# A fused two-layer block on one core: root of the first norm, first masks, one load and the last feature chunk changed, and the written order of all steps replaced

## The chip, the cores and the metric

The kernel runs on one NeuronCore of a Trainium2 chip. The metric is device time in microseconds (us) for one launch. A profiled execution also gives a span, from its first to its last instruction, and every start time below counts from the start of that span. The engines are PE (TensorE, matmuls and transposes), ACT (ScalarE), DVE (VectorE), POOL (GpSimd) and SP (SyncE, which here only issues DMAs). Each engine works through its own instructions in order and waits on semaphores for the others.

## The reference

The input x is 4 x 1024 tokens of 128 features, fp32. There are two layers, each of the form x + s * silu(g), where s comes from an attention and g from a feed-forward network, both fed by a layer norm without learned factors.

```
xn = layernorm(x)                                     # (x - mean) / sqrt(var + 1e-5)
# layer 0, attention: 16 heads of 8, causal, at most 64 back, with a linear bias per head
k, q, v = split(xn @ w_kqv)
s = softmax(q k / sqrt(128) + slope * (key - query), masked) v
# layer 0, feed-forward: weights mixed anew for each of the 4 batches
gate = mean over tokens of (relu(xn gate_w1 + gate_b1) gate_w2 + gate_b2)     # 8 shares
mW1 = W1 + sum_e gate_e TW1_e;  mW2 = W2 + sum_e gate_e TW2_e
g = gelu_tanh(xn mW1 + mb1) mW2 + mb2
x = x + s * silu(g);  xn = layernorm(x)
# layer 1, attention: over the 4 batches at each of the 1024 sites, 16 heads of 8
s = softmax(q k + gated relative bias) v, times Wo, plus bo
# layer 1, feed-forward, hidden size 512; the weights are -1, 0 or 1, with a scale per output
h = silu(w1 xn) * (w2 xn);  h = gelu(h1 h);  h = gelu(h2 h);  g = w3 h
out = x + s * silu(g)
```

## The kernel before

**Units and steps.** The 4096 tokens are worked on in eight units of 512 (`UNITS`: batch and half), numbered 0 to 7. All work is cut into some 1,400 small steps, each a Python function with a short name; `x.02` is the exponential (`x`) of unit 0, tile 2. The string `ORDER` lists all the steps, and `program` calls them in that order. The scheduler is told to keep that order on PE, ACT, DVE and POOL, so each engine's queue is exactly the order in which the steps that use it are written. DMAs are issued by SP in the same way; a DMA issue waits on a semaphore that an earlier transfer raises (there are eight for these queues, taken in turn), so the position of a load in the list also sets which earlier transfer its issue waits for. `PLACES` fixes by hand which buffer each tile takes: eight big SBUF tiles, seven PSUM banks (`ps_M`; digits 3 to 6 only after the scores have ended), four 2 KB tiles (`t2k`) and three streaming tiles (`tw`).

**The bar in ORDER.** What stands before `|` runs first. It ends with a flag (`VF`) that tells whether the fast arithmetic is safe for these weights: norms of the query and key weights (`VN`), and sums over the low halves of the layer-1 weights (`CK.0` to `CK.3`; CK.0 on DVE, the others on ACT). Every engine reads the flag and branches; the fast branch runs the rest, and in the profile it is the one taken. The other branch is an exact version of the same.

**Steps that the change and the prediction speak of, with their lines.** Norm: `ls` statistics (DVE, L411, L413), `lp` root (L418 adds epsilon on DVE or POOL, L419 raises to -0.5 on POOL), `n` scaling (DVE, L426, four instructions), `k` transposes (PE, L432), `K` copy to `xn` (ACT, L437). Layer 0: `q` queries, keys, values (PE, L534 to L537; queries first), `kp` and `kc` older and new keys (POOL; DVE, L555), `FI` ones for the softmax sums (POOL), `m` masked queries (ACT, L571, one 512-wide piece for each of four groups, read from PSUM), `v` values (DVE, L579), `s` scores (PE: L590 adds the additive mask tile `unseen` by small bf16 matmuls, L600 the products), `x` exponential (ACT, L638), `o` weighing (PE, L653), `c`, `p`, `d` copy, turn and divide; `A`, `AR`, `B`, `BP`, `C` the gate; `RW` row weights (PE, L399, from the tile `sb`, then DVE); `E` mixing (DVE, L518: 00 to 07 for mW1, 08 to 0f for mW2 of batch 0); `T` streams expert weights in; `f`, `F`, `g`, `G`, `GS`, `r` the feed-forward. The scores of one tile fill four PSUM banks and there is one such set, so s of the next tile waits for x of the one before it.

Layer 1: `wa`, `wb` and `W`, `U`, `V` are the gated product (PE L756; ACT L767 with a Silu for units 3, 6, 7, L769 with a Tanh for the others; DVE). `ha`, `hb` with `hg`, `hH`, `hL`, and `ia`, `ib` with `ig`, `gH`, `gL`, are the two hidden layers: PE (L810), gelu in place in PSUM (ACT, L820 and L831), a rounded high part (ACT, L826 and L837) and the remainder (DVE, L797). High and low parts go through PE as two fp32r matmuls each, which together keep fp32 accuracy because the weights are exact in fp32r. `j` multiplies by w3 (PE, L845), `J` is the last silu (ACT, L857), `jt` turns it (PE, L864), `y` multiplies (DVE, L869), `Y` adds x and stores (POOL, or DVE for unit 7, L874). `a`, `aq`, `av`, `ag`, ... `ay` are the second attention.

**Table loads.** ACT loads a table whenever its next function is not in the one it has; each such load is one instruction. Exp, gelu, tanh-gelu and silu need different ones; copies, relu and tanh do not force a load.

Of the kernel before, what the change touches and what calls it, by code (L numbers as in the profile page):

```python
# [11 lines left out]
F32 = mybir.dt.float32  # L12
# [9 lines left out]
P = 128  # L22
B, S, D = 4, 1024, 128
H, HD = 16, 8
W = 64
# [27 lines left out]
def constants():  # L53
# [26 lines left out]
    ls.00 lp.00 0. 0. 0. 0. 0. ls.10 lp.10 n.00 k.00 K.00 n.10 q.0 CK.1 m.00 m.03 FI. m.02 kc.0 kp.0 A.00 v.00 v.01 k.10  # L80
    v.02 m.01 K.10 s.00 CK.0 x.00 A.01 AR.01 RW. s.01 VN. AR.00 B.0 CK.3 BP.0 C.0 H.0 E.00 o.00 x.01 s.02 E.01 E.02 CK.2
    E.03 ls.30 E.04 VP. x.02 o.01 E.05 s.03 c.01 D.0 lp.30 x.03 p.01 E.06 d.01 HD.0 E.07 o.02 n.30 o.03 k.30 c.03 kp.1
    p.03 VF. d.03 K.30 | L.1 ls.20 f.10 F.10 q.1 f.00 m.10 lp.20 kc.1 m.12 F.00 m.13 v.11 S.4 f.01 A.11 m.11 f.02 T.00
    n.20 v.10 v.12 F.01 T.01 ls.60 AR.11 f.11 F.02 k.20 S.0 s.10 ls.40 F.11 K.20 T.11 E.08 E.09 f.03 E.0a T.12 S.1 f.12
    lp.40 E.0b E.0c A.10 x.10 AR.10 o.10 E.0d B.1 E.0e s.11 F.03 E.0f n.40 f.13 BP.1 ls.50 lp.60 F.12 C.1 x.11 g.00 T.10
    lp.50 F.13 g.01 E.10 E.11 L.2 k.40 E.12 o.11 n.60 s.12 g.10 G.0 GS.0 n.50 x.12 g.11 E.13 K.40 ls.70 c.11 E.14 k.60
    s.13 r.0 K.60 x.13 A.21 E.15 G.1 ls.01 k.50 p.11 T.16 K.50 o.12 T.13 lp.01 E.16 E.17 T.14 d.11 T.15 E.18 AR.21 o.13
    c.13 D.1 f.20 q.2 F.20 H.1 f.30 E.19 n.01 kc.2 k.01 HD.1 m.20 T.25 m.22 E.1a F.30 f.21 K.01 f.31 m.21 F.21 E.1b F.31
    S.2 f.22 E.1c m.23 kp.2 XH.0 E.1d v.21 f.23 f.32 F.22 F.23 F.32 XL.0 v.20 v.22 wa.00 W.00 U.00 wa.01 wb.00 W.01 V.00
    s.20 wb.01 wa.02 U.01 V.01 T.17 A.20 E.1e E.1f x.20 AR.20 W.02 WH.00 wb.02 lp.70 B.2 s.21 x.21 T.20 g.20 T.24 U.02  # L90
    V.02 wa.03 WH.01 BP.2 WL.00 W.03 C.2 S.3 s.22 o.20 U.03 E.28 E.29 p.13 x.22 n.70 wb.03 o.21 GS.1 s.23 V.03 E.20 d.13
# [12 lines left out]
    m.52 F.43 g.41 ia.20 d.43 s.50 ib.20 G.4 ia.21 k.11 E.36 GS.4 E.3e ib.21 x.50 r.4 K.11 ls.41 ia.22 lp.41 ig.20 ig.21
    n.41 ib.22 gH.20 ig.22 gL.20 gH.21 gL.21 gH.22 s.51 o.50 f.60 gL.22 f.61 F.60 E.37 f.62 F.61 F.62 k.41 E.3f K.41
    XH.4 XL.4 f.50 f.51 F.50 F.51 f.52 F.52 f.53 wa.40 F.53 W.40 f.63 g.50 U.40 wb.40 n.31 F.63 V.40 g.51 wa.41 x.51 G.5
    s.52 WH.40 kp.6 o.51 wa.42 W.41 U.41 wb.41 V.41 a.00 x.52 W.42 s.53 aq.00 WL.40 av.00 wa.43 wb.42 c.51 WH.41 U.42
    p.51 x.53 V.42 o.52 d.51 W.43 WL.41 GS.5 U.43 o.53 c.53 wb.43 WH.42 ia.23 WL.42 V.43 ib.23 p.53 WH.43 d.53 ig.23 q.6
    WL.43 ha.40 kc.6 gH.23 m.60 gL.23 hb.40 j.20 v.60 ha.41 r.5 m.61 v.61 ls.51 hb.41 hg.40 m.62 hH.40 m.63 j.21 hg.41
# [38 lines left out]

DIRECT = (3, 6, 7)


AHEAD = ("FI", "q", "kp", "kc", "m", "v", "s", "x", "o", "c", "p", "d")


PLACES = {
    "big": (
        "0123456780325416724531806738426710526370847015623701601505842374206142658371437121268263756047510763"
        "48253017620317485"  # L160
# [7 lines left out]
        "01230123012301230123012301203120302130321"  # L168
    ),
    "tw": (  # L170
        "012201010200210120212010"
    ),
}

# [952 lines left out]
```

## Time and profile before

| | |
|---|---|
| median of 3 runs | 419.1 us (418.81 to 420.6) |
| the profiled execution: time, span | 418.97 us, 416.9 us |
| granted TensorE clock | 0.994 |
| busy: PE, ACT, DVE, POOL | 395.4, 352.3, 329.1, 165.8 us |
| table loads on ACT | 73, 1283 ns each |
| DMA | 26.42 MB, most of it in the first 25 and around 34 to 100 us |

Of the profile's views, the page gives busy time by engine and the span in 40 slices of 10.4 us (a digit is the busy share in tenths). The chain follows the work that ended last back from the end: start, duration, engine and line. The timeline lists instructions in order of their start, merged where neighbours are alike: start, busy time, engine, line, operation, output and input, shape, count, and in square brackets how long the engine stood idle before it and what ended that. ACT_TABLE_LOAD is a table load. A matmul of fp32 operands shows as two instructions.

### The profile page before, as it was taken

The numbers are of one execution on the slowest core, as the hardware profiler recorded it, in microseconds if no ns is written. First come the engines' busy times: TensorE is split into PE (matmuls) and PEld (weight loads), VectorE is DVE, ScalarE is ACT, GpSimd is POOL, SyncE is SP. The second block draws the span as 40 slices with busy tenths as digits, with TensorE's granted clock in tenths as the row PEclk, the third lists the DMA queues.
The fourth block names the chain that finished last, engine by engine and source line by source line (L and its number), as shares of the span: only waits on it lengthen the run. The fifth ranks groups of instructions, "written<-read, shape, count | busy, mean of one in ns | idle before, by whom it ended". The sixth has DMA issues, their size and how long they took to land.

```text
span 416.9 us, 11388 instructions
## 1 busy us (share of the span) xinstructions
PE 395.4 (95%) x4800; PEld 281.6 (68%) x4800; DVE 329.1 (79%) x704; ACT 352.3 (85%) x489; POOL 165.8 (40%) x186
## 2 busy tenths in 40 slices
PE   7779999999999999999999999999998998999992
PEld 3445686587767676757786678666786876788881
DVE  6687999787859985344565699799899999999992
ACT  1867997998979999798988899999979898988973
POOL 5012154257211530221442253462565564555462
PEclk9999999999999999999999999999999999999997
DMA  7926544332014441000000000000000000000013
GB/s 278 350 99 240 217 132 151 108 108 93 6 50 129 130 163 39 2 2 2 3 1 3 2 2 0 3 2 2 2 0 0 3 0 0 2 1 25 2 75 109
DMA packets 8891, 26.42 MB, mean 63 GB/s; under 512 B 1248, under 2 KB 2048, under 8 KB 8448
## 3 DMA queue, kind: packets, MB, share of 16 engines
q1 hardware_dynamic: 8112, 23.79, 16.7%
q10 hardware_dynamic: 720, 1.84, 1.2%
q8 instruction: 39, 0.64, 0.6%
q14 instruction: 20, 0.16, 0.1%
HBM read 23.52 MB, written 2.10 MB: 61 GB/s over the span
## 4 chain that ended last, share of the span: by engine, by line
PE 72%; ACT 14%; DVE 5%; DMA 4%; issue 3%; POOL 0%; SPq 0%; ACTq 0%; DVEq 0%; POOLq 0%
PE ps_M L810 21%; PE ps_S L600 7%; PE ps_M L756 7%; PE ps_M L696 6%; PE ps_O L653 6%; PE ps_M L713 6%; PE ps_M L898 5%; PE ps_M L845 3%; PE ps_S L590 2%; ACT big L638 2%; DMA g<-in_l1h 2%; DVE mw L518 2%; ACT L820 2%; PE ps_M L432 1%; PE ps_M L670 1%
## 5 line engine op out<-in xcount | busy, mean ns | idle before, releaser
L810 PE MATMUL ps_M<-big,l1h 128*128 128x512 f32 x512 | 130.1, 399 | 2.6 <-ACT ps_M L477 1.0
L810 PEld LDWEIGHTS ps_M<-big,l1h 128*128 128x128 f32 x512 | 94.1, 188 | 26.8 <-issue 2.0
L638 ACT ACTIVATE big<-ps_S 128x2048 f32<-128x2048 f32 x32 | 60.2, 1880 | 13.0 <-PE ps_S L600 12.9
L797 POOL TENSOR_TENSOR big<-t2k,big 128x512 fp32r<-128x512 f32 x32 | 44.6, 1402 | 52.5 <-ACT big L788 39.3
L797 DVE TENSOR_TENSOR big<-ps_M,big 128x512 fp32r<-128x512 f32 x64 | 43.1, 684 | 8.7 <-ACT big L837 4.5
L600 PE MATMUL ps_S<-big,k 32*64 32x256 f32 (+1 forms) x768 | 36.5, 462 | 1.0 <-issue 1.0
L419 POOL TENSOR_TENSOR rstd<-rstd,power 128x4 f32<-128x4 f32 x16 | 18.3, 1145 | 47.5 <-DVE rstd L418 46.7
L518 DVE SCALAR_TENSOR_TENSOR mw<-tw,gr,mw 128x512 f32<-128x512 f32 x42 | 36.1, 869 | 0.5
L653 PEld LDWEIGHTS ps_O<-big,vb 128*32 128x32 f32 x2048 | 29.8, 110 | 9.2 <-issue 7.2
L653 PE MATMUL ps_O<-big,vb 128*32 128x64 f32 x2048 | 34.0, 220 | 0.6 <-ACT big L638 0.6
L756 PE MATMUL ps_M<-xh,l1w 128*128 128x512 f32 x64 | 31.7, 495 | 1.6 <-ACT t2k L767 1.6
L696 PE MATMUL ps_M<-xn,mw 128*128 128x512 f32 x64 | 31.4, 608 | 0.8 <-DVE inv L682 0.6
L713 PEld LDWEIGHTS ps_M<-mw,big 128*128 128x128 f32 x256 | 29.8, 192 | 2.5 <-issue 1.1
L984 POOL TENSOR_TENSOR big<-big 128x512 f32<-128x512 f32 x16 | 22.4, 1407 | 22.8 <-DVE big L974 22.8
L713 PE MATMUL ps_M<-mw,big 128*128 128x128 f32 x256 | 30.9, 277 | 0.0
L898 PE MATMUL ps_M<-wa,xn 128*128 128x416 f32 x64 | 26.5, 523 | 1.2 <-ACT vb L910 1.1
L728 POOL TENSOR_TENSOR g<-g,s 128x512 f32<-128x512 f32 x8 | 11.5, 1435 | 38.6 <-ACT g L723 30.4
L600 PEld LDWEIGHTS ps_S<-big,k 32*64 32x64 f32 x768 | 18.6, 130 | 11.6 <-issue 8.8
L756 PE MATMUL ps_M<-xl,l1w 128*128 128x512 f32 x64 | 25.2, 394 | 0.0
L782 DVE SCALAR_TENSOR_TENSOR t2k<-ps_M,halved,t2k 128x512 f32<-128x512 f32 x20 | 14.9, 748 | 12.0 <-PE ps_M L756 11.7
L820 ACT ACTIVATE ps_M<-ps_M,vec 128x512 f32<-128x512 f32 x32 | 21.2, 667 | 3.2 <-PE ps_M L810 3.1
L451 POOL TENSOR_TENSOR xl<-xn,xh 128x512 fp32r<-128x512 f32 x8 | 11.4, 1420 | 31.6 <-DVE xh L443 26.1
(185 smaller groups left out, 840.8 us busy)
## 6 DMA issues: line engine op xcount, KB each, us to landing
tw<-in_tw SPq DMA_DIRECT2D x24, 512.0 KB, 4.0
big<-in_tw SPq DMA_DIRECT2D x2, 1024.0 KB, 7.1
out<-xn SPq DMA_DIRECT2D x7, 256.0 KB, 2.0
g<-in_l1h ACTq DMA_DIRECT2D x2, 512.0 KB, 7.9
g<-in_l1h SPq DMA_DIRECT2D x2, 512.0 KB, 8.6
x<-in_tw SPq DMA_DIRECT2D x2, 512.0 KB, 4.7
x<-in_x SPq DMA_DIRECT2D x1, 1024.0 KB, 6.8
x<-in_x ACTq DMA_DIRECT2D x2, 256.0 KB, 3.8
```

Of the source, the lines that this page charges most:

```text
L518: DVE.scalar_tensor_tensor(m, part, made["gr", b][:, e:e + 1], base if e == 0 else m, ALU.mult, ALU.add)
L600: PE.matmul(sp[rows, j, :, q0:q0 + n], lhsT=k[r, key:key + W], rhs=qm[r, :, t * P + q0:t * P + q0 + n], start=bool(exact), stop=bool(exact ...
L638: ACT.activation(pr, sp, AF.Exp)
L653: PE.matmul(op[32 * j:32 * j + 32, part, qs], lhsT=vb[:, col:col + 32], rhs=pr[:, j, g, qs], start=(odd + i + g == 0), stop=(odd + i + g = ...
L696: PE.matmul(hp, lhsT=made["mixed", b][0][:, c * P:(c + 1) * P], rhs=xn[:, b, cx], start=True, stop=True)
L713: PE.matmul(op[:, i, :], lhsT=hid[:, c, i * P:(i + 1) * P], rhs=m2[:, c * D:(c + 1) * D], start=(c + i == 0), stop=(c + i == FC + 2))
L756: PE.matmul(p, lhsT=wt[name][:, c * P:(c + 1) * P], rhs=m, start=(n == 0), stop=(n == len(both) - 1))
L797: engine.tensor_tensor(made[key + "l", u][:, c, :], made[key + "v", u, c], made[key + "h", u][:, c, :].bitcast(F32), ALU.subtract)
L810: PE.matmul(made[name, u, c], lhsT=wt[name][:, i, c * P:(c + 1) * P], rhs=m[:, i, :], start=(n + i == 0), stop=(last and i == FC - 1))
L820: ACT.activation(full, full, AF.Gelu, scale=v("h1s", c))
L898: PE.matmul(mp[:, 0:N_ALL], lhsT=xn[:, b, place(sl)], rhs=wa[:, 0:N_ALL], start=True, stop=True)
L984: POOL.tensor_tensor(pv[:, t:t + 2, 0:2, :], pv[:, t:t + 2, 0:2, :], pv[:, t:t + 2, 2:4, :], ALU.add)
```

## The change

1. **Order.** All of `ORDER` is new, and `PLACES` with it. The diff shows its beginning up to a little past the bar, and its end. Which steps stand before the bar is the same, apart from the new `M` steps and `kp.1`, which goes behind it.
2. **Root.** Only for the first norm (unit 0, first layer): Sqrt of the variance plus epsilon on ACT (epsilon from a new tile set by POOL), then a reciprocal on DVE. The warming instruction on ACT, which loaded a table with a copy, is now a Sqrt. Exp therefore needs a load of its own before x.00.
3. **Masks of unit 0.** `m.0g` writes only the 128 columns that s.00 reads; a new step `M.0g` writes the other 384.
4. **Load.** The DMA of `unseen` is issued behind `wg` and ahead of a raw h1 half, instead of behind `tb`.
5. **Last chunk.** For unit 7, chunk 3 (`LAST`), the second gelu writes an fp32 SBUF tile; its high part and remainder are not made, and `j.73` is one fp32 matmul (two instructions) instead of two fp32r ones.

```diff
 ORDER = """
-    ls.00 lp.00 0. 0. 0. 0. 0. ls.10 lp.10 n.00 k.00 K.00 n.10 q.0 CK.1 m.00 m.03 FI. m.02 kc.0 kp.0 A.00 v.00 v.01 k.10
-    v.02 m.01 K.10 s.00 CK.0 x.00 A.01 AR.01 RW. s.01 VN. AR.00 B.0 CK.3 BP.0 C.0 H.0 E.00 o.00 x.01 s.02 E.01 E.02 CK.2
-    E.03 ls.30 E.04 VP. x.02 o.01 E.05 s.03 c.01 D.0 lp.30 x.03 p.01 E.06 d.01 HD.0 E.07 o.02 n.30 o.03 k.30 c.03 kp.1
-    p.03 VF. d.03 K.30 | L.1 ls.20 f.10 F.10 q.1 f.00 m.10 lp.20 kc.1 m.12 F.00 m.13 v.11 S.4 f.01 A.11 m.11 f.02 T.00
...
-    aT.6 y.20 j.62 jt.00 aU.6 jt.50 gH.72 aD.71 ay.5 af.6 at.7 gL.63 y.50 aT.7 aU.7 jt.10 j.63 J.60 ay.6 gL.70 af.7 y.00
-    gL.71 ia.73 ib.73 Y.50 ig.73 ay.7 Y.20 U.63 y.10 jt.30 gL.72 gH.73 jt.60 y.30 gL.73 j.70 j.71 y.60 j.72 Y.00 Y.10
-    Y.30 Y.60 j.73 J.70 jt.70 y.70 J.71 jt.71 y.71 U.73 Y.70 Y.71
+    0. ls.00 lp.00 n.00 0. ls.10 0. 0. k.00 0. K.00 q.0 m.00 m.03 m.02 M.00 m.01 M.03 lp.10 VN. M.01 kc.0 M.02 n.10 FI.
+    CK.0 A.00 k.10 RW. v.01 kp.0 v.00 s.00 K.10 x.00 A.01 AR.01 AR.00 v.02 B.0 s.01 H.0 BP.0 o.00 C.0 CK.3 E.00 E.01
+    E.02 E.03 E.04 ls.30 lp.30 D.0 x.01 s.02 o.01 CK.1 x.02 HD.0 s.03 n.30 E.05 CK.2 c.01 p.01 VP. x.03 E.06 o.02 VF.
+    E.07 o.03 c.03 k.30 d.01 K.30 p.03 d.03 | T.00 f.10 f.00 ls.20 F.00 lp.20 T.01 q.1 f.11 n.20 F.10 L.1 T.10 kp.1 m.10
+    f.01 kc.1 k.20 v.10 F.11 m.13 F.01 f.02 A.11 K.20 A.10 F.02 AR.11 T.12 f.12 m.11 m.12 f.03 E.08 E.09 E.0a E.0b E.0c
+    AR.10 s.10 E.0d E.0e f.13 v.11 B.1 E.0f ls.60 F.12 F.03 BP.1 g.00 g.01 C.1 lp.60 T.11 x.10 v.12 s.11 E.10 n.60 F.13
+    E.11 g.10 G.0 o.10 T.13 x.11 GS.0 E.12 E.13 s.12 E.14 E.15 E.16 E.17 x.12 T.14 g.11 r.0 ls.40 o.11 S.1 E.18 s.13
+    c.11 G.1 f.20 x.13 lp.40 ls.01 p.11 lp.01 o.12 o.13 E.19 k.60 D.1 d.11 T.15 E.1a n.01 F.20 c.13 S.0 n.40 f.21 E.1b
...
+    gL.63 ay.5 gH.70 aT.6 y.50 aD.70 j.62 ig.72 aU.6 at.7 j.63 gH.71 jt.00 af.6 gL.70 aT.7 J.60 Y.50 ay.6 aU.7 y.00
+    jt.20 Y.00 jt.30 gL.71 U.33 y.20 j.70 Y.20 af.7 jt.60 ia.73 gH.72 ib.73 j.71 ay.7 y.30 y.60 gL.72 Y.30 jt.10 Y.60
+    j.72 y.10 ig.73 j.73 J.70 gL.73 jt.70 gH.73 U.63 Y.10 J.71 jt.71 y.70 y.71 Y.70 Y.71
...
 
@@ -151,24 +151,27 @@
 DIRECT = (3, 6, 7)
 
 
-AHEAD = ("FI", "q", "kp", "kc", "m", "v", "s", "x", "o", "c", "p", "d")
+LAST = (7, 3)
+
+
+AHEAD = ("FI", "q", "kp", "kc", "m", "M", "v", "s", "x", "o", "c", "p", "d")
 
 
 PLACES = {
...
 }
@@ -259,6 +262,7 @@
     nc.sync.dma_start(out=raw["h2"][:, 0:2 * F], in_=a["l1h2"][:, 0:2 * F])
     nc.scalar.dma_start(out=raw["h2"][:, 2 * F:4 * F], in_=a["l1h2"][:, 2 * F:4 * F])
     nc.sync.dma_start(out=wg, in_=a["wg"])
+    nc.sync.dma_start(out=unseen, in_=a["unseen"])
     nc.sync.dma_start(out=raw["h1"][:, 0:2 * F], in_=a["l1h1"][:, 0:2 * F])
     nc.scalar.dma_start(out=raw["h1"][:, 2 * F:4 * F], in_=a["l1h1"][:, 2 * F:4 * F])
     nc.sync.dma_start(out=sb, in_=a["sb"])
@@ -266,7 +270,6 @@
     nc.sync.dma_start(out=raw["w1"], in_=a["l1w1"])
     nc.sync.dma_start(out=raw["w2"], in_=a["l1w2"])
     nc.sync.dma_start(out=tb.rearrange("p c e -> p (c e)"), in_=a["tb"])
-    nc.sync.dma_start(out=unseen, in_=a["unseen"])
     nc.sync.dma_start(out=w1, in_=a["w1"])
 
     def v(name, i=0, n=1):
@@ -284,6 +287,8 @@
     POOL.memset(power, -0.5)
     one = const.tile([P, 1], F32, tag="one", name="one")
     POOL.memset(one, 1.0)
+    eps = const.tile([P, 1], F32, tag="eps", name="eps")
+    POOL.memset(eps, 1e-5)
     flag = tmp.tile([1, 1], I32, tag="flag", name="flag")
     made = {"nrm": small([P, 2 * H + 4], "nrm")}
 
@@ -315,7 +320,7 @@
     nc.sync.dma_start(out=w2, in_=a["w2"])
     nc.sync.dma_start(out=vec[:, early_n:V_N], in_=a["vec"][:, early_n:V_N])
     warm = const.tile([P, 1], F32, tag="warm", name="warm")
-    ACT.copy(warm, one)
+    ACT.activation(warm, one, AF.Sqrt)
     in_order = {mybir.EngineType.PE, mybir.EngineType.Activation, mybir.EngineType.DVE, mybir.EngineType.Pool}
 
     def tokens(u):
@@ -415,6 +420,10 @@
         @step("lp")
         def ln_power(u, i):
             rstd = made["rstd", u, i] = small([P, 4], "rstd")
+            if (u, i) == (0, 0):
+                ACT.activation(rstd, made["mv", u, i][:, :, 1], AF.Sqrt, bias=eps)
+                DVE.reciprocal(rstd, rstd)
+                return
             (POOL if i else DVE).tensor_scalar(rstd, made["mv", u, i][:, :, 1], 1e-5, None, ALU.add)
             POOL.tensor_tensor(rstd, rstd, power, ALU.pow)
 
@@ -568,7 +577,12 @@
         def mask(u, g):
             if ("qm", u) not in made:
                 made["qm", u] = big((P, 4, U))
-            ACT.activation(made["qm", u][:, g, :], made["qp", u], AF.Copy, scale=mpart[:, g:g + 1])
+            cols = slice(0, P if u == 0 else U)
+            ACT.activation(made["qm", u][:, g, cols], made["qp", u][:, cols], AF.Copy, scale=mpart[:, g:g + 1])
+
+        @step("M")
+        def mask_rest(u, g):
+            ACT.activation(made["qm", u][:, g, P:U], made["qp", u][:, P:U], AF.Copy, scale=mpart[:, g:g + 1])
 
         @step("v")
         def value(u, i):
@@ -794,6 +808,8 @@
                 return
             if c == 0:
                 made[key + "l", u] = big((P, FC, U), wide)
+            if (key, u, c) == ("l", *LAST):
+                return
             engine.tensor_tensor(made[key + "l", u][:, c, :], made[key + "v", u, c], made[key + "h", u][:, c, :].bitcast(F32), ALU.subtract)
 
         steps["WL"] = lambda u, c: low(POOL, "w", u, c)
@@ -827,19 +843,24 @@
 
         @step("ig")
         def last_gelu(u, c):
-            full = made["lv", u, c] = made["h2", u, c]
-            ACT.activation(full, full, AF.Gelu, scale=v("h2s", c))
+            full = made["lv", u, c] = t2k() if (u, c) == LAST else made["h2", u, c]
+            ACT.activation(full, made["h2", u, c], AF.Gelu, scale=v("h2s", c))
 
         @step("gH")
         def last_high(u, c):
             if c == 0:
                 made["lh", u] = big((P, FC, U), wide)
+            if (u, c) == LAST:
+                return
             ACT.copy(made["lh", u][:, c, :], made["lv", u, c])
 
         @step("j")
         def last_out(u, c):
             if c == 0:
                 made["j", u] = bank()
+            if (u, c) == LAST:
+                PE.matmul(made["j", u], lhsT=wt["w3"][:, c, :].bitcast(F32), rhs=made["lv", u, c], start=False, stop=True)
+                return
             both = halves("l", u)
             for n, m in enumerate(both):
                 PE.matmul(made["j", u], lhsT=wt["w3"][:, c, :], rhs=m[:, c, :], start=(n + c == 0), stop=(c == FC - 1 and n == len(both) - 1))
```

## The prediction

> **What bounds the kernel now.** I read the page's slices first, then the chain of work that ended last, then the timeline at the two ends, then the waits of PE in between. The slices show PE full nearly everywhere; it falls short in the first three slices (0 to 31 us) and the last one.
>
> ```profile
> PE   7779999999999999999999999999998998999992
> ACT  1867997998979999798988899999979898988973
> ```
>
> PE's 395.4 us of busy time leave 21.5 us of the 416.9 us span. The stretches I asked for put about 8 us of it before 33.94 us, where the branch begins, 7.9 us after 405 us, and some 6 us in the 371 us between. A new order can shorten only these three.
>
> The chain, its head (start, us, what):
>
> ```profile
> 2.11 8.50 DMA g<-in_l1h
> 10.99 4.02 DMA unseen<-in_unseen
> 15.50 1.22 PE ps_S L600 x16
> 16.79 1.73 issue
> ...
> 23.83 1.03 issue
> ...
> 31.08 1.15 PE ps_O L653 x64
> 33.94 1.10 PE ps_M L696 x2
> ```
>
> The end goes back through s.00 to the load of the mask tile `unseen`, which was issued only when the raw h1 half on ACT's queue had landed. "Issue" is time in which PE waited for nothing that the profile shows. The timeline there:
>
> ```profile
> 5.60 1.28 ACT L318 ACT_TABLE_LOAD   x1 [5.60 <-DMA cst<-in_const]
> ...
> 6.79 2.37 DVE L426 TENSOR_SCALAR nt<-x,mv,rstd 128x128 f32<-128x128 f32 x8
> ...
> 9.38 1.13 PE L534 MATMUL ps_S<-xn,wqkv 128*128 128x512 f32 x2 [0.67 <-ACT xn L437]
> ...
> 10.70 1.91 ACT L376 ACTIVATE big<-g 128x2048 f32<-128x2048 uint16 x1 [1.36 <-DMA g<-in_l1h]
> ...
> 12.60 2.40 ACT L571 ACTIVATE big<-ps_S,cst 128x512 f32<-128x512 f32 x4
> ...
> 15.06 0.44 PE L590 MATMUL ps_S<-unseen 32*32 32x512 bf16 x16 [1.50 <-DMA unseen<-in_unseen]
> ```
>
> So s.00 waited for two things that came together: the tile, landed at 15.01, and the four query masks, done at 15.00 because CK.1 stood before them on ACT. The tail:
>
> ```profile
> 403.01 2.08 PE L810 MATMUL ps_M<-big,l1h 128*128 128x512 f32 x8
> ...
> 405.15 1.28 ACT L831 ACT_TABLE_LOAD   x1 [1.11 <-issue]
> ...
> 406.45 0.66 ACT L831 ACTIVATE ps_M<-ps_M,vec 128x512 f32<-128x512 f32 x1
> 407.14 0.58 ACT L837 CAST big<-ps_M 128x512 fp32r<-128x512 f32 x1
> 407.75 1.28 ACT L857 ACT_TABLE_LOAD   x1
> ...
> 408.51 0.49 PE L845 MATMUL ps_M<-big,l1w 128*128 128x512 f32 x1 [0.23 <-DVE big L797]
> 409.04 0.84 ACT L857 ACTIVATE g<-ps_M,vec 128x256 f32<-128x256 f32 x2
> ```
>
> PE ends ib.73 at about 405.05; then table, gelu, cast, table, silu (J.70) run one after another. In the built kernel's instruction list, which names each wait, this gelu's table load itself carries the waits on PE and DVE, so it cannot run ahead. In the middle, PE's waits are on ACT, mostly for a PSUM bank; the two longest:
>
> ```profile
> 315.41 0.97 PE L898 MATMUL ps_M<-wa,xn 128*128 128x416 f32 x2 [1.12 <-ACT vb L910]
> 349.36 0.50 PE L756 MATMUL ps_M<-xh,l1w 128*128 128x512 f32 x1 [1.57 <-ACT t2k L767]
> ```
>
> **The change, part by part.**
>
> Root by ScalarE. Removed: DVE's add (0.17) and the first of POOL's two powers (2.29 us for two). Added: a Sqrt behind the table load and the warming instruction on ACT, then a reciprocal. Load to 6.88, warming 0.19, sqrt about 0.2 (the 192 ns row), reciprocal 0.14 (the 128x8 row), handoffs: scaling starts near 7.45 instead of 6.79, +0.65. Bounds: 0, if the DMA issues ahead of the load on ACT go out sooner, to +1.0. One of PE's idle matmuls now follows k.00 and can add 0.1, so q.0 starts near 10.1 instead of 9.38. The Sqrt also needs the eps memset on POOL (0.1, by 2.9 us: hidden).
>
> Exp now needs its own load before x.00. It stands behind K.10 and carries no wait, so it runs while ACT waits for s.00: K.10 ends near 15.1, the load (1.28) near 16.4, s.00 near 16.7. Cost 0, cover 0.3. The Trainium skill (ScalarE: Activation LUTs, "What ACT_TABLE_LOAD costs") puts a switch of sets at about 2.66 us with the drain, and the rule in its section "Table sets: the hidden batching unit" is to batch calls by set, which speaks against a lone Sqrt. By that figure x.00 would be an estimated 1.1 us later and the forecast 417.8. The rows here show 1.28 us with the next instruction 0.02 us behind (405.15, 406.45), and the sum goes by them.
>
> Masks in two steps. CK.1 leaves its place before the masks. Four 128-wide pieces (266 ns, the 128x128 copy) and one 384-wide (478 ns) stand before s.00: 1.55 us from 11.25, so 12.8 instead of 15.00. The other three pieces run under PE's work.
>
> Mask tile sooner. SP issues `unseen` after wg, near 4.6 instead of 10.99; it stops binding. Queued behind it on SP: the raw h1 half, near 5.2 instead of 4.57, and sb. By the instruction list sb's issue now waits for vec (landed 7.94), so 7.98 instead of 5.40; the load issued at 7.98 before, l1w1, took 5.8 to 6.0 us, so sb lands near 13.8.
>
> What is late next for s.00. In the new order n.10 follows kc.0 on DVE, and RW stands before s.00 on PE. kc.0 12.15 to 12.85; n.10 four by 0.296, to 14.05; k.10 to 14.45; RW's four matmuls, to 15.0. VN (1.1) now precedes kc.0 on DVE, but it runs from 10.1 to 11.2 while DVE waits for the keys; FI and kp.0 (0.75 and 0.55 on POOL) follow lp.10's power, end near 12.5 and hide under n.10; CK.0 (2.29) moves ahead of the values, which o.00 needs only after 20. So s.00 starts near 15.0: gain 0.05. The tile, the masks and the root together save nothing by themselves.
>
> From s.00 to the branch. Before, PE lost 1.03 in the middle of s.02 (the second "issue" line), so x.02 began at 25.57. New: x.00 16.7, x.01 20.4 to 22.3, CK.1 (2.1) on ACT to 24.35, x.02 to 26.2, CK.2 (1.28) and c.01 (0.48) under s.03, x.03 28.0 to 29.9, against 31.03: gain 1.1, or 0.2 if the stall comes back. DVE's work for f.10 from 20.96 (eight mixes by 0.75, statistics 1.23, scaling 1.1, bias, row and flag 1.9) ends near 31.3, before p.03 does; it hides. The flag is made before E.07 instead of after p.03, so the branch costs some 0.15 less. I take 0.8 for the head, between the two cases; bounds 1.5 gained to 0.4 lost.
>
> Tail. gelu 7,3 writes an SBUF tile and its table load carries no wait in the new list, so it loads while PE works. Cast and subtraction of that chunk go; the fp32 matmul is two instructions by 0.43 to 0.5 in place of two by 0.23. PE work moved ahead of ib.73: jt.30, jt.60 (0.44 each), j.70 (0.46), less jt.10 (0.44): 0.9 later. After it: j.71, jt.10, j.72 are 1.36, gelu is ready at +0.75, j.73 ends at +2.3, the silu's load at +2.05; J.70 at +2.35. Before +4.0, now 0.9 + 2.35 = 3.25: gain 0.75. Bounds: 0 (PE starved by ACT there) to 1.3, the load.
>
> Middle, from 34 to 405. PE's work there is the same. PE's waits of over 0.2 us that name an engine are 0.97, 0.28, 0.69, 0.22, 0.46, 1.12, 1.57 and 0.50, 5.8 together, seven of eight on ACT. Counting the lists, table loads in the branch go from 72 to 69 (3.85 us of ACT), and those that carry a wait, and so cannot run ahead, from 20 to 16 with the tail's. In proportion to the latter (15 of 19) the waits shrink by 1.2, in proportion to all loads by 0.25; I take 0.7, between them. Bounds: 3.5 gained (a little over half the waits) to 4.7 lost (first rival). The moved transfers of the branch (both tw2 halves ahead of x) hide: T.00 and T.01 feed E.08, which comes some 6 us of DVE work into the branch.
>
> Sum: 0.8 + 0.75 + 0.7 = 2.25. The profiled execution took 418.97 (span 416.9 and 2.07 around it), 0.13 under the median of 419.1. 418.97 - 2.25 = 416.7.
>
> **The rivals.**
>
> Slower: the gated units' table loads. Silu for W is loaded 8 times instead of 5, and the longest wait, 1.57 at 349.36, is PE waiting for just such a W (a gelu, a load, then the silu that frees the bank). If the three more each stall PE by 1.57 and nothing else shrinks: 4.7, less 1.55 of the ends, 422.1. It decides from two such stalls on, which undo the ends and more. Against it: the loads that carry waits are fewer.
>
> Row weights late: RW stands before s.00, and if sb takes the 8.1 us that it took before, from 7.98, it lands at 16.1, s.00 starts near 16.7, 1.65 late. With the tail's 0.75 and no other gain: 419.9.
>
> Nothing to measure: DVE is the fuller engine from 50 to 72 us (21.34 of 22). PE reaches the branch earlier, DVE less so, PE waits for n.01 before k.01 (its cover in the trace is 69.89 to 71.27, 1.4), and only the tail remains: 418.2.
>
> More: a better packing takes most of the middle's waits, 3.5: 413.9.
>
> **How the numbers follow.** Forecast 0.40, silu loads 0.18, row weights 0.09, only the tail 0.18, more 0.15. A measurement of this kernel can tell about 0.5% (2.1 us) from no change. The forecast lies at that edge, so 0.32 of its 0.40 counts as faster (its sum is uncertain on the lower side too) and 0.08 as same; with "more" that is 0.47 faster, 0.35 same, 0.18 slower. The range reaches from the "more" case, a little widened, 413.0, to the slower rival, 422.0; the forecast's own is 415 to 418.5.
>
> **What would show it.** Right: s.00 near 15.0 with no wait for `unseen`; x.03 ending near 30; the branch's first matmul near 33.1; no table load between ib.73's end and the last gelu; J.70 about 2.35 behind ib.73; fewer and shorter waits of PE on ACT between 300 and 365. Wrong: PE waiting for sb before L404 (the RW line of the new kernel); x.00 waiting for its table; PE waits on the W line that sum to over 4 us; a stall at k.01.

## The result: 412.6 us, and where the 7 us lie

The changed kernel takes 412.56 us (median of 6 runs, 412.45 to 415.04) against 419.79 us for the kernel before on the same chip (6 runs, 418.81 to 420.63): a ratio of 0.984, 95% interval 0.982 to 0.986. The forecast was 416.7 us with a range from 413.0 to 422.0. The direction was right, the size three times too small, and the time lies 0.44 us below the range.

The page of the changed kernel, busy time in 40 slices of 10.3 us and under it the clock that was granted to TensorE:

```profile
PE   7879999999999999999999999999999999999992
ACT  2875997999989999998988988878996999976972
PEclk9978999999999999999999999999999999999997
```

The two 8s that PE had in slices 31 and 34 are gone. One thing in this page belongs to this execution alone: the windows view gives a granted clock of 0.50 in one stretch of the head (start and end, length, then busy time and count of PE, PEld, DVE, ACT, POOL; then the granted clock, DMA share and GB/s).

```profile
27.00:33.00 6.00, 5.75 (x136) 3.90 (x139) 4.51 (x16) 3.48 (x5) 0.17 (x1) 0.50 0.01 3
```

So the branch's first matmul is at 35.57 here, and the profiled execution took 415.04 us while four of the other five took 412.45 to 412.65. The runs e4, e9 and e10 below have the same work ahead of the bar at a clock of 1.00; in them that matmul starts at 33.00 to 33.61. I therefore measure the body of each kernel from that first matmul of the branch.

The head, in the timeline (start, busy time, engine, line, operation, output and input, shape, count, idle time before it and what ended that):

```profile
14.73 0.43 PE L604 MATMUL ps_S<-unseen 32*32 32x512 bf16 x16
14.80 1.28 ACT L652 ACT_TABLE_LOAD   x1
...
16.41 1.88 ACT L652 ACTIVATE big<-ps_S 128x2048 f32<-128x2048 f32 x1 [0.32 <-PE ps_S L614]
...
24.62 0.65 PE L614 MATMUL ps_S<-big,k 32*64 32x256 f32 x5 [1.09 <-issue]
```

s.00 no longer waits for the mask tile, the added load of the exp table runs while PE makes the scores, and the stall inside s.02 is back, 1.09 us.

The body. Windows of the kernel before, then of the run e3 (the changed body at full clock), both cut at 300 us; the columns are those of the windows view above:

```profile
34.00:300.00 266.00, 263.17 (x3827) 183.76 (x3828) 200.84 (x461) 238.93 (x312) 98.33 (x104) 1.00 0.19 62
300.00:402.00 102.00, 98.75 (x468) 77.61 (x467) 96.87 (x154) 88.08 (x144) 53.61 (x60) 1.00 0.01 3
```

```profile
34.00:300.00 266.00, 265.81 (x3845) 186.71 (x3844) 200.07 (x468) 241.88 (x316) 101.23 (x107) 1.00 0.18 61
300.00:402.00 102.00, 100.89 (x482) 78.66 (x480) 98.43 (x152) 87.59 (x143) 61.50 (x64) 1.00 0.04 13
```

PE's idle time, the length less its busy time, falls from 2.83 to 0.19 us up to 300 us and from 3.25 to 1.11 us behind: 4.8 us. What the changed kernel's own trace still shows between 100 and 402 us are five short waits, the longest three:

```profile
343.82 0.50 PE L770 MATMUL ps_M<-xh,l1w 128*128 128x512 f32 x1 [0.26 <-ACT t2k L781]
...
354.02 2.11 PE L826 MATMUL ps_M<-big,l1h 128*128 128x512 f32 x8 [0.33 <-DVE big L813]
...
366.07 0.66 PE L885 MATMUL ps_M<-cst,g 128*128 128x128 f32 x4 [0.22 <-DVE big L813]
```

What the prediction left out is ACT's own idle time ahead of its table loads. These are loads of the kernel before, with the time that ACT stood still ahead of them:

```profile
102.74 1.28 ACT L820 ACT_TABLE_LOAD   x1 [1.15 <-PE ps_M L810]
...
171.38 1.28 ACT L723 ACT_TABLE_LOAD   x1 [2.53 <-DVE g L719]
...
286.81 1.28 ACT L767 ACT_TABLE_LOAD   x1 [0.74 <-PE ps_M L756]
...
308.35 1.28 ACT L820 ACT_TABLE_LOAD   x1 [1.03 <-PE ps_M L810]
...
345.35 1.28 ACT L820 ACT_TABLE_LOAD   x1 [1.22 <-PE ps_M L810]
```

With 1.29 at 68.27, 0.35 at 272.59 and 0.55 at 300.53 that is 8.9 us between the branch's first load and the tail. In the changed kernel three loads of that stretch are left with such idle time, 1.05, 0.87 and 0.24: 2.2 us.

The tail of the changed kernel:

```profile
399.59 1.28 ACT L847 ACT_TABLE_LOAD   x1
...
400.50 2.10 PE L826 MATMUL ps_M<-big,l1h 128*128 128x512 f32 x8
...
402.64 0.69 ACT L847 ACTIVATE t2k<-ps_M,vec 128x512 f32<-128x512 f32 x1 [1.77 <-PE ps_M L826]
...
403.35 1.28 ACT L878 ACT_TABLE_LOAD   x1
...
403.80 1.02 PE L862 MATMUL ps_M<-t2k,l1w 128*128 128x512 f32 x2
404.86 0.84 ACT L878 ACTIVATE g<-ps_M,vec 128x256 f32<-128x256 f32 x2 [0.23 <-PE ps_M L862]
```

The gelu's table is loaded at 399.59 while PE still works; ib.73 ends at 402.60, the last silu starts 2.26 us later. Before, it was 3.95 us.

### The profile page after: what moved, and what is told of

It is laid out like the page before. It is cut to its first block, busy times and chain, and to the rows that moved or that the text cites. A ratio compares the mean times of both kernels' runs of the same rounds, so it can differ in the third digit from the quotient of the medians.

```text
span 413.2 us, 11394 instructions
## 1 busy us (share of the span) xinstructions
PE 398.1 (96%) x4800; PEld 283.2 (69%) x4800; DVE 325.7 (79%) x703; ACT 351.5 (85%) x491; POOL 167.7 (41%) x186
## 4 chain that ended last, share of the span: by engine, by line
PE 79%; DVE 11%; ACT 4%; issue 3%; POOL 1%; DVEq 0%; POOLq 0%; ACTq 0%
PE ps_M L826 21%; PE ps_S L614 8%; PE ps_O L667 7%; PE ps_M L710 7%; PE ps_M L727 7%; PE ps_M L770 6%; PE ps_M L919 3%; PE ps_M L866 3%; PE ps_S L604 3%; DVE big L813 2%; PE ps_V L546 2%; PE ps_M L364 2%; PE ps_S L543 2%; PE ps_M L544 2%; DVE vb L971 2%
## 5 line engine op out<-in xcount | busy, mean ns | idle before, releaser
L826 PE MATMUL ps_M<-big,l1h 128*128 128x512 f32 x512 | 134.1, 405 | 0.6 <-DVE big L813 0.3
L813 POOL TENSOR_TENSOR big<-t2k,big 128x512 fp32r<-128x512 f32 x32 | 42.3, 1332 | 57.1 <-ACT big L802 51.4
L667 PEld LDWEIGHTS ps_O<-big,vb 128*32 128x32 f32 x2048 | 31.3, 113 | 8.4 <-issue 5.1
L667 PE MATMUL ps_O<-big,vb 128*32 128x64 f32 x2048 | 35.6, 225 | 0.0
L428 POOL TENSOR_TENSOR rstd<-rstd,power 128x4 f32<-128x4 f32 x15 | 15.5, 1032 | 49.1 <-DVE rstd L427 34.7
L1005 POOL TENSOR_TENSOR big<-big 128x512 f32<-128x512 f32 x16 | 23.5, 1476 | 21.0 <-DVE big L995 21.0
L742 POOL TENSOR_TENSOR g<-g,s 128x512 f32<-128x512 f32 x8 | 10.2, 1278 | 51.4 <-DVE s L702 35.3
L770 PE MATMUL ps_M<-xh,l1w 128*128 128x512 f32 x64 | 30.4, 474 | 0.3 <-ACT t2k L781 0.3
L847 ACT ACTIVATE ps_M<-ps_M,vec 128x512 f32<-128x512 f32 x31 | 20.3, 666 | 5.5 <-PE ps_M L826 5.4
L717 ACT ACTIVATE big<-ps_M,mb 128x512 f32<-128x512 f32 x32 | 21.6, 694 | 2.6 <-PE ps_M L710 2.2
L836 ACT ACTIVATE ps_M<-ps_M,vec 128x512 f32<-128x512 f32 x32 | 21.3, 668 | 2.4 <-PE ps_M L826 1.8
```

Of the source, the lines that this page charges most:

```text
L667: PE.matmul(op[32 * j:32 * j + 32, part, qs], lhsT=vb[:, col:col + 32], rhs=pr[:, j, g, qs], start=(odd + i + g == 0), stop=(odd + i + g = ...
L717: ACT.activation(made["hid", u][:, c, :], made["f", u, c], AF.Gelu_apprx_tanh, bias=made["mixed", b][2][:, c:c + 1])
L770: PE.matmul(p, lhsT=wt[name][:, c * P:(c + 1) * P], rhs=m, start=(n == 0), stop=(n == len(both) - 1))
L813: engine.tensor_tensor(made[key + "l", u][:, c, :], made[key + "v", u, c], made[key + "h", u][:, c, :].bitcast(F32), ALU.subtract)
L826: PE.matmul(made[name, u, c], lhsT=wt[name][:, i, c * P:(c + 1) * P], rhs=m[:, i, :], start=(n + i == 0), stop=(last and i == FC - 1))
L1005: POOL.tensor_tensor(pv[:, t:t + 2, 0:2, :], pv[:, t:t + 2, 0:2, :], pv[:, t:t + 2, 2:4, :], ALU.add)
```

## The experiments

Twelve kernels were run, each beside the kernel before. The table holds the ratio of times and, from each run's trace, the stretch from the branch's first matmul (its start) to the end of ib.73, and from there to the start of J.70. No kernel leaves out work; the line numbers of a run are those of its own text, so that L580 in e5 or L594 in e2 is the mask tile's line, L590 before.

| kernel | ratio to before (95% interval) | first matmul at | to ib.73's end | to J.70 |
|---|---|---|---|---|
| before | 1 | 33.94 | 371.15 | 3.95 |
| changed | 0.984 (0.982 to 0.986) | 35.57 | 367.03 | 2.26 |
| e1 new head, old body | 0.999 (0.997 to 1.001) | 33.35 | 371.60 | 3.97 |
| e2 old head, new body | 0.982 (0.978 to 0.986) | 33.09 | 367.49 | 2.26 |
| e3 root by POOL again | 0.981 (0.977 to 0.985) | 33.13 | 366.94 | 2.28 |
| e4 last chunk as before | 0.982 (0.977 to 0.987) | 33.00 | 367.00 | 2.81 |
| e5 old order, three words moved | 0.999 (0.997 to 1.001) | 33.54 | 371.00 | 3.96 |
| e6 old order, eight early loads | 0.986 (0.983 to 0.988) | 33.70 | 367.17 | 2.96 |
| e7 both of these | 0.990 (0.988 to 0.993) | 33.62 | 369.27 | 2.93 |
| e8 changed, twelve loads more | 1.008 (1.006 to 1.011) | 33.48 | 377.69 | 2.25 |
| e9 changed, three early loads | 0.984 (0.981 to 0.986) | 33.61 | 366.48 | 2.27 |
| e10 changed, four loads more | 0.988 (0.986 to 0.991) | 33.51 | 369.54 | 2.26 |
| e11 old order, early loads, two words moved | 0.988 (0.985 to 0.990) | 32.92 | 365.62 | 2.94 |
| e12 as e11, last chunk in fp32 | 0.986 (0.983 to 0.989) | 32.99 | 366.83 | 3.17 |

### Head or body (e1, e2)

e1 takes all of the change ahead of the bar, root, masks and mask tile included, and keeps the old list behind it:

```diff
-    <words of before, up to the bar> | L.1 ls.20 f.10 F.10 ...
+    <words of the change, up to the bar> | kp.1 L.1 ls.20 f.10 F.10 ...
-LAST = (7, 3)
+LAST = (99, 99)
```

> The new order, loads, root and masks before the bar; behind the bar the old order and places, and the last chunk as before. Theory (the gain sits behind the bar, in PE waits that the new order does not have): only the head's share comes, 0.8 to 1.0 us, so a ratio near 0.998. Rival (the earlier start of the branch is what lets the rest run without waits): most of the 6.8 us comes, ratio 0.985 to 0.99.

Measured: 419.48 us, ratio 0.999. The head alone gives nothing that can be told from noise; the interval (0.997 to 1.001) leaves room for the 0.8 us, but not for the rival's 0.985 to 0.99.

e2 is the other half: the old words ahead of the bar, with POOL's power, masks in one piece and the mask tile behind `tb`, and the new words behind it without kp.1.

> The mirror image: head as before (order, power on POOL, masks in one piece, late mask tile), the new order behind the bar and the last chunk in fp32. Theory: 5.5 to 6 us of the gain, ratio 0.986 to 0.987, and the eight PE waits on ACT of over 0.2 us (5.8 us together) nearly gone from its profile. Rival: 1.5 us or less, ratio 0.996 or more, with waits as before.

Measured: 412.70 us, ratio 0.982, all of the gain and more than the theory's 5.5 to 6 us. PE's waits of 0.2 us and more sum to 0.97 us between the branch's first matmul and ib.73, against 5.8 before. Its trace has a lesson on the head too. It runs the old head, yet its s.00 starts 0.93 us sooner than in the profile before, because the mask tile landed sooner:

```profile
14.13 0.44 PE L594 MATMUL ps_S<-unseen 32*32 32x512 bf16 x16 [0.50 <-DMA unseen<-in_unseen]
```

Over the traces with the old head (before, e2, e5, e6, e7, e11, e12) the branch's first matmul starts at 32.92 to 33.94, mean 33.40; over those with the new head at full clock and the root by ScalarE (e1, e4, e8, e9, e10) at 33.00 to 33.61, mean 33.39. The late tile, which I had counted as the bound of the head, was in part an accident of the one execution that I read.

### Root and last chunk undone (e3, e4)

e3 gives the first norm POOL's power again:

```diff
-            if (u, i) == (0, 0):
+            if (u, i) == (99, 0):
-    ACT.activation(warm, one, AF.Sqrt)
+    ACT.copy(warm, one)
```

> The changed kernel with the first norm's root by POOL's power again, and the warming copy. If the root on ACT delays the head as its trace shows (scaling from 7.81 against 6.79): up to 1.0 us faster than the changed kernel, about 411.6, ratio 0.982. If s.00 waits for something else: the same as the changed kernel, 412.5, ratio 0.984.

Measured: 412.12 us, ratio 0.981. The two cases differed by 0.002, less than the interval: whether the root costs the head a few tenths stays open. s.00 starts at 14.30 in e3 and at 14.46 to 14.89 in e4, e8, e9 and e10.

e4 makes the last chunk as before, in two parts:

```diff
-LAST = (7, 3)
+LAST = (99, 99)
-    ... ig.73 j.73 J.70 gL.73 jt.70 gH.73 U.63 ...
+    ... ig.73 gH.73 gL.73 j.73 J.70 jt.70 U.63 ...
```

> The changed kernel with the last chunk as before (gelu in PSUM, rounded part, remainder, two fp32r matmuls), in the new order. If the tail gains as its trace shows (2.28 us from the end of ib.73 to J.70 against 3.99 before): 1.7 us slower than the changed kernel, 414.2, ratio 0.988. If the order alone gave the tail: no more than 0.5 us slower, ratio 0.985.

Measured: 412.64 us, ratio 0.982. I had expected 1.7 us; that fell. The tail of e4:

```profile
397.02 1.28 ACT L837 ACT_TABLE_LOAD   x1
...
400.04 0.66 ACT L837 ACTIVATE ps_M<-ps_M,vec 128x512 f32<-128x512 f32 x1 [1.74 <-PE ps_M L816]
...
402.81 0.84 ACT L868 ACTIVATE g<-ps_M,vec 128x256 f32<-128x256 f32 x2 [0.19 <-PE ps_M L856]
```

The gelu works in place again, and its load still ran 3 us ahead. In the instruction list of e4 this load waits for DVE alone, in that of before for DVE and PE. So the early load belongs to the order, not to the fp32 chunk, whose own worth by these two traces is 2.81 - 2.26 = 0.55 us.

### What made PE's waits in the middle: three words moved (e5)

Each of three long waits of PE in the kernel before ended with an instruction of ACT that stood behind a table load. e5 moves those three words ahead of it:

```diff
-    ... m.30 hg.00 r.2 ha.01 AR.31 hb.01 ...
+    ... m.30 AR.31 hg.00 r.2 ha.01 hb.01 ...
-    ... ib.21 x.50 r.4 K.11 ls.41 ...
+    ... ib.21 K.11 x.50 r.4 ls.41 ...
-    ... hb.12 hg.11 av.51 ad.21 ...
+    ... hb.12 av.51 hg.11 ad.21 ...
```

Two of these waits in the trace of the kernel before (the third, at 315.41, is shown in the prediction):

```profile
105.45 0.73 PE L810 MATMUL ps_M<-big,l1h 128*128 128x512 f32 x2 [0.97 <-ACT ps_M L477]
...
177.02 1.87 PE L810 MATMUL ps_M<-big,l1h 128*128 128x512 f32 x7 [0.69 <-ACT xn L437]
```

> The kernel before with three words of its order moved and nothing else: AR.31 ahead of hg.00, K.11 ahead of x.50, av.51 ahead of hg.11. Each of the three frees a PSUM bank that PE waits for (0.97 us at 105.45, 0.69 at 177.02, 1.12 at 315.41 in the profile before), and each stood behind a table load and the function that needed it. Theory (the waits in the middle are made by a few words of ACT in the wrong place): the three waits go and nothing takes their place, 2.8 us off, ratio 0.993, 0.7 or less left of the three waits. Rival (PE waits because ACT as a whole is full, and a wait taken away comes back at the next bank): under 1 us off, ratio 0.998 to 1.000.

Measured: 419.84 us, ratio 0.999. The sum fits the rival, but the trace shows another thing. At 105 us the wait of 0.97 became one of 0.23 and at 315 us the wait of 1.12 is gone, for good; the third move was wrong. ACT and PE of e5 around 177 us:

```profile
174.10 0.59 ACT L427 COPY xn<-ps_M 128x512 f32<-128x512 f32 x1 [2.13 <-PE ps_M L422]
174.71 1.28 ACT L628 ACT_TABLE_LOAD   x1
176.00 1.88 ACT L628 ACTIVATE big<-ps_S 128x2048 f32<-128x2048 f32 x1
```

```profile
177.93 0.44 PE L580 MATMUL ps_S<-unseen 32*32 32x512 bf16 x16 [1.08 <-ACT big L628]
...
181.72 2.63 PE L686 MATMUL ps_M<-xn,mw 128*128 128x512 f32 x5 [1.27 <-DVE big L787]
```

Now K.11 makes ACT wait 2.13 us for PE, and the load of the exp table stands behind that. PE then waits 2.35 us for what follows, in place of 0.69.

### The loads run early (e6)

e6 keeps the old order and all 73 loads. It adds a step that applies a function of the wanted table to one column of a constant, 0.20 us, behind the last ACT instruction ahead of each of eight loads; so the load is issued by an instruction that waits for nobody.

```diff
+        @step("tl")
+        def table_load(i):
+            ACT.activation(warm, one, (AF.Exp, AF.Gelu, AF.Silu, AF.Gelu_apprx_tanh)[i])
...
-    ... v.32 ls.11 m.30 hg.00 ...
+    ... v.32 ls.11 m.30 tl.1 hg.00 ...
-    ... J.60 ay.6 gL.70 af.7 y.00 gL.71 ia.73 ib.73 Y.50 ig.73 ...
+    ... J.60 tl.1 ay.6 gL.70 af.7 y.00 gL.71 ia.73 ib.73 Y.50 ig.73 ...
```

(The others: ahead of F.20, GS.4, W.30, W.32, hg.10 and hg.31.)

> The kernel before with eight one-column activations on a constant added (0.2 us each), each ahead of an instruction that waits for another engine and needs a new table: F.20, hg.00, GS.4, W.30, W.32, hg.10, hg.31, ig.73. The number of loads stays; each of these eight now runs while ACT waits. Theory (a load that stands behind a wait is what costs): the waits at 105.45 (0.97), 288.84 (0.46), 315.41 (1.0 of 1.12), 349.36 (1.2 of 1.57) go and the tail's gelu is 1.1 sooner: 4.7 us off, ratio 0.989. Rival (the waits come back elsewhere): only the tail's 1.1, ratio 0.997.

Measured: 413.95 us, ratio 0.986 (0.983 to 0.988), some nine tenths of what the whole change gains. ACT of e6 at hg.00, where ACT stood still 1.15 us ahead of the load in the kernel before, and at ig.73:

```profile
102.04 1.28 ACT L349 ACT_TABLE_LOAD   x1
103.34 0.20 ACT L349 ACTIVATE warm<-one 128x1 f32<-128x1 f32 x1
103.45 0.64 ACT L814 ACTIVATE ps_M<-ps_M,vec 128x512 f32<-128x512 f32 x1
...
399.84 1.28 ACT L349 ACT_TABLE_LOAD   x1
401.14 0.20 ACT L349 ACTIVATE warm<-one 128x1 f32<-128x1 f32 x1
401.25 0.64 ACT L825 ACTIVATE ps_M<-ps_M,vec 128x512 f32<-128x512 f32 x1
```

PE's wait at 105 us is gone; the matmuls run through:

```profile
101.80 6.50 PE L804 MATMUL ps_M<-big,l1h 128*128 128x512 f32 x27
```

The waits of 0.69, 0.46, 1.12 and 1.57 are 0, 0, 0.24 and 0.46. From the branch's first matmul to ib.73 it takes 4.0 us less than before, and 1.0 less from there to J.70, with the same number of loads of the same length; 4.7 in all had been expected. What cost this time in the old order was that a load which carries another engine's semaphore starts only when that engine is done.

### Both, and both without K.11 (e7, e11)

e7 has e5's three moves and e6's early loads; e11 has the early loads and the moves of AR.31 and av.51 only.

> The kernel before with both edits, the three moved words and the eight early table loads. Theory: 2.8 + 4.7, less the 2.0 that they share (105.45 and 315.41): 5.5 us off, ratio 0.987, so most of what the new order gains. Rival: 1.1 to 1.5 us off, ratio 0.997.

> The kernel before with the eight early table loads and two of the three moved words: AR.31 and av.51 moved, K.11 left where it was. Theory (the move of K.11 alone made the waits of 1.08 and 1.27 us at 178 and 182, since x.50 then stood behind K.11): those two waits are gone, 2 us faster than with all three words, 413.7, ratio 0.985. Rival (any local move pushes the wait elsewhere): as with all three words, 0.990.

e7 measured 416.01 us, ratio 0.990, between the theory and the rival: adding the three moves to the early loads loses 2.1 us from the first matmul to ib.73 (369.27 against 367.17), with the same waits of 1.07 and 1.28 us at 178 and 182. In e11 these two are absent and the stretch is 365.62 us; the mechanism of e5's failure is shown. The time of e11 is less clear. Its trace is of its shortest run, 411.79 us; the median is 414.09 us, ratio 0.988, between what the theory and the rival had expected. Its longest run, 415.65 us, had a mean granted clock of 0.986, against 0.992 to 0.995 in the others; what the other four lose, 1.3 to 2.4 us, no trace shows.

### The number of loads (e8, e10)

Behind 300 us the kernel before has 24 loads and the changed one 20 (e3's trace); up to there 48 and 49. e8 adds twelve loads to the changed kernel at six places, e10 four at two of these:

```diff
-    ... gH.11 ...
+    ... tl.0 gH.11 ...
-    ... ig.60 ...
+    ... tl.0 ig.60 ...
```

(This is e10. e8 has these two, `tl.0` ahead of ig.03 and gH.23, and `tl.1` ahead of WH.00 and hH.53.)

> The changed kernel with twelve table loads more: six one-column activations of another set, each in the middle of a run of one set (Exp ahead of ig.03, gH.23, gH.11 and ig.60, gelu ahead of WH.00 and hH.53), so that each makes two loads; 15.4 us more of ACT. Theory (places, not number): PE stays covered nearly everywhere, 0 to 2 us slower than the changed kernel, ratio to the kernel before 0.982 to 0.987. Rival (the gain comes from the three loads fewer, so from how full ACT is): twelve more take all of the 4.7 us of the middle back, ratio 0.994 or more.

> The changed kernel with four table loads more behind 300 us, where its list has four fewer than the list before: the two Exp activations ahead of gH.11 and ig.60, 5.5 us of ACT. In the run with twelve more, the work behind the last exponential of layer 0 fell back from 8.7 to 10.8 us. Theory (behind 300 us ACT has room for about half of it): 2.0 us slower than the changed kernel, ratio to the kernel before 0.987. Rival one (the loads fewer are the whole gain there): all 5.5 us, 0.995. Rival two (they cost only because ACT was late already): nothing, 0.982.

e8 measured 423.42 us, ratio 1.008: 15.4 us of loads cost 10.7 us of time (to ib.73, 377.69 against 366.94 in e3), and the theory that their number hardly matters fell. Following the exponentials of layer 0 through both traces, the delay against e3 goes from 0.4 to 3.2 us at the first place, to 6.1 at the second, 7.7 at the third, and 8.7 at the fourth. ACT of e8 at the first place:

```profile
87.24 1.88 ACT L646 ACTIVATE big<-ps_S 128x2048 f32<-128x2048 f32 x1
89.14 1.28 ACT L354 ACT_TABLE_LOAD   x1
90.43 0.20 ACT L354 ACTIVATE warm<-one 128x1 f32<-128x1 f32 x1
90.54 2.17 ACT L796 CAST big<-t2k 128x512 fp32r<-128x512 f32 x4
92.72 1.28 ACT L646 ACT_TABLE_LOAD   x1
94.02 1.88 ACT L646 ACTIVATE big<-ps_S 128x2048 f32<-128x2048 f32 x1
```

The second exponential in e3:

```profile
90.71 1.89 ACT L652 ACTIVATE big<-ps_S 128x2048 f32<-128x2048 f32 x1
```

There is no gap in e8 from 87.24 to 95.9: between these two exponentials of unit 2 (x.21 and x.22) ACT has no slack, and the two loads move the second from 90.71 (e3) to 94.02, later by 2.9 us after the head's difference of 0.4. PE then waits 1.66 us for it (95.95). e10 measured 414.45 us, ratio 0.988, so 2.0 us more than the changed kernel, as worked out for it; behind 300 us PE's idle time went from 1.11 to 2.35 us, with a new wait of 0.61 us for ACT at 330.76 the longest. (To ib.73's end it is 2.6 us more than in e3. Half of that is idle time of PE; the other half lies in its busy time, 367.00 us against 365.63 for the same 4,317 matmul records, and why these take longer is not shown.) So a load has two prices: what it holds up by itself where ACT is full, 0.5 to 1.5 us of time each in these two runs, and what ACT stands still ahead of it when it waits.

How the new order's gain splits between the two is not shown. To ib.73 the changed kernel is 4.1 us shorter; e6 gets 4.0 us with no load fewer, e10 loses 2.6 us by four loads more, and these are not the places at which the old order had its four. The new placement of the PSUM banks (`PLACES`) came with the order, and no run tells the two apart.

The Trainium skill (ScalarE: Activation LUTs, "Table sets: the hidden batching unit") advises to group calls by set and do all of one set before switching. e8 and e10 agree with it in direction. Where a switch stands was worth about 4 us of the body in e6, with no load fewer.

### Early loads in the new order, and the fp32 chunk in the old one (e9, e12)

e9 puts early loads ahead of the three loads of the changed kernel that still have idle time before them: `tl.1` ahead of ha.03 (for hg.03) and ahead of ig.52, `tl.2` behind gH.53 (for W.32).

> The changed kernel with its three remaining loads that stand idle before they start run early: a one-column activation each ahead of hg.03, ig.52 and W.32 (1.03, 0.87 and 0.25 us of idle ACT ahead of these loads in the changed order). Theory (early loads gain only where PE waits for what stands behind them; in the new order PE waits for none of these three): 0.3 us or less, ratio to the kernel before as the changed kernel's, 0.980 to 0.985. Rival (each us of ACT idle ahead of a load is a us of the end): 2.2 us faster, ratio 0.977.

Measured: 412.09 us, ratio 0.984 (0.981 to 0.986), as the changed kernel; the rival's 0.977 lies outside the interval. Of the 2.2 us of idle ACT the traces show at most 0.5 in the end: to ib.73 it takes 366.48 us, against 366.94 in e3. So idle time of ACT ahead of a load matters where PE later waits for it, and in the changed kernel PE had no wait over 0.2 us behind these three loads.

e12 adds `LAST = (7, 3)` and its code to e11.

> The kernel before, its own order, with the eight early table loads, two moved words (AR.31, av.51) and the change's fp32 product for the last chunk; nothing else of the change. From the branch's first matmul to the last silu the old order with the first two edits took 368.6 us, the changed kernel's pieces 369.0 to 369.3. Theory (the new order as such is not needed, only what it does to ACT's table loads, and the fp32 product is worth 0.5 us): 368.0 us between these two points, time as the changed kernel's within 1 us, ratio 0.981 to 0.985. Rival (the whole new order is needed): 0.987 or more.

Measured: 413.70 us, ratio 0.986; between the two cases, so it settles little. In the old order the fp32 product gains nothing: J.70 comes 3.17 us behind ib.73 instead of 2.94, since j.70, j.71 and j.72 still stand ahead of it on PE. The other 1.2 us against e11 is lost between 57 and 80 us, by the starts of the exponentials. Around there the trace has two waits of PE, 0.32 us at 47.09 and 0.28 at 65.95, that it puts down to "issue"; e6 has the same two and loses 0.7 us in the same places against the kernel before, 1.1 against e11, and e11 has neither. The last section has a lead on these waits. No variant was shown to be faster than the changed kernel.

## Why the prediction was too small

**Head, 0.8 us forecast: not there.** s.00 came at 14.73 (forecast 15.0), the exp table hid, the branch's first matmul came at 33.0 to 33.6 at full clock (forecast 33.1). The forecast of the new head lay in its scatter, at the early end, and what it was compared with was the late end of the old head's scatter: 33.94, mean 33.40. By the means nothing is gained, and e1's ratio is 0.999. The "issue" stall in s.02, whose absence I had counted in the better case, came back at 1.09 us. The root's scaling started at 7.81 instead of the forecast 7.45: the table load began 0.28 us later and the Sqrt took 0.28 instead of 0.2. The rival "row weights late" did not happen: `sb` was issued at 5.92 us, not at the 7.98 counted on, and landed near 12.7; L404 began at 14.09 with no wait for it.

**Tail, 0.75 us forecast: 0.8.** J.70 came 2.26 us behind ib.73, forecast 2.35; less the 0.9 us of PE work moved ahead, the gain against 3.95 is 0.8. The split was wrong in one point: I had put the early load down to the SBUF tile, and e4 shows it without that tile.

**Middle, 0.7 us forecast, at most 3.5: about 4.8.** This is the term that failed, and its size, not its mechanism. By PE's idle time it is 4.8 us; by the stretch from the first matmul to ib.73, 371.15 - 367.03 = 4.1 us, with the 0.9 us of moved work (the prediction's count) on top 5.0 us. I had named the right objects, waits of PE on ACT and loads that carry waits, but scaled the sum of the waits by how many such loads there are (15 of 19). That step failed: the waits of 0.2 us and more fell from 5.8 to 0.8 us, not by a fifth. A count says nothing of which loads matter: e6 took the waits off eight of twenty and 4.0 us went. The list of loads with idle time ahead of them, 8.9 us, was in the trace and would have shown that waits and loads belong together one by one. And my bound of 3.5, "a little over half the waits", rested on nothing: all 5.8 us of waits could go. With that bound the low end is 418.97 - (0.8 + 0.75 + 5.8) = 411.6, and the range holds the result. The rival "more", 413.9, came nearest, though 0.8 of its gain was a head that is not there.

**The rival "silu loads".** It feared 1.57 us for each more silu load ahead of W. The W line's longest wait in the changed kernel is 0.26 us (343.82). But its ground was sound: e8 shows that a pair of loads more costs up to 2.9 us where ACT is full. Behind 300 us, where the new order has four loads fewer, ACT is the less full (busy 0.86 of the time before, against 0.90 ahead of 300), and there four loads more cost 2.0 us in e10.

**What is not accounted for.** Middle and tail sum to 5.6 us, the medians differ by 7.2. 0.8 of the rest is that the profiled execution before (418.97) lies under the median of its six runs here (419.79). Another 0.3 lies outside the span: a run's time less its span is 2.1 us on average for the kernel before and 1.8 for the changed one, 1.76 to 1.81 in all runs with the new body and 2.03 to 2.24 in those with the old; the prediction had taken its 2.07 as fixed, and why it falls no run shows. The remaining 0.5 us I cannot place: the other runs left no trace, and the "issue" waits, the landing of the first transfers and the stretch behind J.70 (7.0 to 8.4 us) differ between the traces by as much or more.

## What to carry to other kernels

Before costing a new order, list every table load of ScalarE with the idle time ahead of it, and for each ask whether TensorE later waits for something behind it: those waits are what starting the loads early can win. The number of loads counts too, 0.5 to 1.5 us for each added one here. Where only such a load is in the way, a one-column activation of the same table behind the last instruction that doesn't wait brings the load forward for 0.2 us, without touching the order. Bound a gain by all of the waits that exist, and take the start of a head from several traces when it hangs on a transfer.

## What was unexpected in the hardware

The granted TensorE clock fell to 0.50 from 27 to 33 us in one execution of the changed kernel, after a stretch in which PE was busy 1.68 of 3 us (24 to 27 us), and cost 2.0 to 2.6 us (35.57 against 33.00 to 33.61). How thin that stretch was does not decide it: e9 with the same head was busy as little there and kept 1.00.

```profile
24.00:27.00 3.00, 1.68 (x69) 1.22 (x70) 2.62 (x14) 1.68 (x1) 0.84 (x1) 0.97 0.03 8
```

```profile
24.00:27.00 3.00, 1.68 (x69) 1.22 (x70) 2.75 (x15) 1.56 (x2) 0.68 (x1) 1.00 0.04 11
```

(The changed kernel, then e9.) The Trainium skill (TensorE: Matmul & The Clock Gate, "Part 1: The HAM clock gate") describes such a half rate after an idle window of about 3.4 us, with a window that runs free of the kernel; the value agrees, and that it struck one of several alike executions fits the free-running window, but the stretch here was thin rather than idle, and why it struck is not shown.

A switch of tables cost ACT 1.28 us and no more: in e6 the next function starts 0.02 us behind the load (102.04 + 1.28, 103.34), and in the changed kernel x.00 started 0.33 us behind the end of its load, when its scores were done. The 2.66 us with the drain that the Trainium skill gives (ScalarE: Activation LUTs, "What ACT_TABLE_LOAD costs") did not appear in any row here.

The "issue" waits have a lead in the profile's packets. The 14 traces have 19 such waits of PE over 0.2 us between 14 us and the end, one of 0.6 to 1.2 us in s.02 in every trace and the five of 0.2 to 0.33 in e1, e6 and e12. Each of the 19 ends 2.2 to 2.6 us after the start of a 16 KB packet on the queue that the page lists as q8, instruction (39 packets, 0.64 MB). So PE may have been waiting for its own instructions there; no run tests it.
